# Four graph layers on one core: a projection's place in the third layer, score banks and last roots in the fourth

## The chip, the core and the metric

The kernel runs on one core of a Trainium2 chip. The metric is the device time of one execution in microseconds (us); lower is better. A core has five engines that run side by side and wait for one another by semaphores: TensorE (PE, matrix products into PSUM), VectorE (DVE), ScalarE (ACT), GpSimd (POOL) and SyncE (SP, which here only issues transfers). Each works its own list of instructions in the order in which it was given.

## The reference

Four attention layers over the same graph of 4096 nodes with 256 features, each with a residual and a layer norm. Cut to what matters for this change:

```python
# layer 1 (L0): additive attention, 4 heads, leaky slope 0.2, elu
# layer 2 (L1): 4-head dot-product attention, mask added before the softmax
# layer 3 (L2): additive attention, one head
h = x @ W
e = leaky(h @ a[:D] + (h @ a[D:]).T, 0.01)
attention = softmax(where(adj > 0, e, MASK_VAL), axis=1)
x = layernorm(x + elu(attention @ h))
# layer 4 (L3): cosine attention, values are the features themselves
Qn, Kn = cos_normalize(x @ Wq.T), cos_normalize(x @ Wk.T)
att = softmax(where(adj > 0, Kn @ Qn.T, NEG), axis=1)
x = layernorm(x + 0.5 * (att @ x) + 0.5 * x)
```

## The kernel before

The 4096 nodes are cut into 32 tiles of 128 rows. Four tiles of result rows make a block (512 columns of the transposed score matrix), so each layer runs over eight blocks, 0 to 7; within a block it runs over the 32 tiles of source nodes, in the third and fourth layer two at a time: sixteen pairs, numbered g = 0 to 15.

**Third layer** (`additive_one`). `weights(b, g)` makes the unnormalised weights of a pair: ScalarE computes a rectified row (L566) into one of two PSUM banks of the pool `pr`, VectorE turns it with the mask into `prob` (L567). From block 1 on the product with the features is done with seven half-size products instead of eight; for it VectorE (L436) and GpSimd (L437, L438) form the differences `mix`. `sums` issues the products (L446) into the four banks of `pa`, three pairs behind the weights (`LAG = 3`). After a block's last product, ScalarE and VectorE read the four banks out as `quarters` (L451 to L460), VectorE's first reading at L452; the next block's first products wait for that.

The block before is finished meanwhile: `finish(b - 1, g)` is called once in each pair. It has four row tiles k to take care of. `project` multiplies the quarters with the layer's weights (L596, four matmuls) into a bank of the pool `ps`, which has two. `take` reads that bank: a reciprocal on VectorE (L602), then an exponential and a rectification on ScalarE (L604, L605). `add` completes elu, residual and the row's statistics on VectorE (L613, L614, L156, L157). Roots and scaling follow at g = 10, 11, 14 and 15. The list of pairs in which each is called stands in `finish` by hand, since in this layer the order on TensorE, VectorE and ScalarE is the order of the program (`manual_schedule`).

Two blocks behind, the fourth layer's rows are prepared with `follow.prepare`, a generator of which one step is run in most pairs. Its matmuls L1063, at g = 8, take both banks of `ps`. Its later steps read them by ScalarE (L1070), make roots (L1073, `first_root` on ScalarE, `end_root` on GpSimd at L1076) and scale the rows (L1079).

During block 0 of the third layer, the last block of the second layer is completed by the generator `tail` (called `before` there), nineteen steps: two additions of denominators (L867), row sums on TensorE (L880) with their copies (L883), a transposition (L888), reciprocals (L903), two halves (L895, L909, L912), four row statistics, roots (on GpSimd at the end), four scalings, factors. Three steps run in each pair from g = 4.

**Fourth layer** (`cosine_attention`). `scores` multiplies a tile pair (L1118) into a bank: of `pz` (two banks), or, after block 0, of `ps` for odd tiles; ScalarE takes the exponential (L1122), VectorE the mask (L1130). The products are L446 again, four tiles behind. `pa` holds the four accumulators; the pools are opened in the order pa, pz, ps and lie in PSUM in this order, where the third layer had pr, pa, ps. Each block's `y` starts as 1.5 times the features (L1272), of which two buffers exist; `outputs_far` completes a block during the next (L1165 to L1176 and the store L1182). The third layer's last block is completed by its own tail at the start of this layer. Here a planner orders the instructions by its own estimates, apart from the end, `ending(7)`, which is in program order on TensorE, VectorE and ScalarE: for rows k = 0 to 3 it adds the last four tiles directly (`direct`, L1202) and the quarters (`others`, L1208), sums a row on ScalarE (`twice_sum`, L1213), scales and takes statistics on VectorE (`row`, L1216, L1176 to L1179), makes the roots two rows at a time (`begin_root`, `end_root`: L182, L161, L162, L168 to L171), scales by ScalarE (L1222) or VectorE (L186) and stores.

Of the kernel before, what the change touches and what calls it, by code (L numbers as in the profile page):

```python
# [9 lines left out]
FP = mybir.dt.float32  # L10
# [4 lines left out]
OP = mybir.AluOpType  # L15
# [13 lines left out]
def kernel(  # L29
# [32 lines left out]
    def pool(stack, name, bufs, **kw):  # L62
        return stack.enter_context(tc.tile_pool(name=name, bufs=bufs, reuse_waits="tile", **kw))
# [463 lines left out]
    def additive_one(w_sb, ga, tail, op, follow):  # L527

        with ExitStack() as lay:
# [87 lines left out]
            def finish(b, g):  # L617


                if g in (1, 2, 4, 6):  # L620
                    project(bank, b, g // 2)
                if g in (2, 3, 5, 7):
                    take(sb, b, g // 2 if g > 2 else 0)
                if g in (3, 4, 6, 8):
                    add(b, g // 2 - 1)
                elif g == 10:
                    roots[b] = begin_root(mvs[b])
                elif g == 11:
                    v, r, n = roots[b]
                    end_root(v, r, n, nc.gpsimd)  # L630
                    nc.gpsimd.tensor_tensor(v, mvs[b][:, :, 0], r, OP.mult)
                    nc.gpsimd.tensor_scalar(v, v, -1.0, 1.0, OP.mult, OP.add)
                elif g in (14, 15):
                    v, r, _ = roots[b]
                    for k in (2 * g - 28, 2 * g - 27):
                        y = ys[b][:, k, :]
                        nc.scalar.activation(y, y, AF.Identity, bias=v[:, k:k + 1], scale=r[:, k:k + 1])
                if g == 15:
                    if b < NB - 2:
                        far_y[b] = saved.tile([P, QB, D], FP, name=f"far_y{b}")  # L640
                        nc.scalar.dma_start(far_y[b], ys[b])
                    else:
                        nc.scalar.dma_start(X[:, b * QB:(b + 1) * QB, :D], ys[b])
# [5 lines left out]
            with tc.manual_schedule(engines=fixed):  # L649
                for i in range(len(units) + LAG):  # L650
                    b, g = units[i - LAG] if i >= LAG else (-1, 0)
                    if g == NP - 1:
                        sums(b, g)
                    if i < len(units):
                        weights(*units[i])
                    if b >= 0:
                        if g < NP - 1:
                            sums(b, g)
                        if b:
                            finish(b - 1, g)  # L660
                        else:
                            for _ in range(3 if g > 3 else 0):
                                next(before, None)
                            if g == 11:
                                follow.start()
                            elif g == 14:
                                follow.centre(bank())
                            if g % 2:
                                t = mixed[g // 2] = keep.tile([P, 2, 4, P], FP, name=f"mixed{g // 2}")
                                mix_features(t, g // 2)  # L670
                        if b > 2 and g == 0:
                            follow.prepare(bank, b - 3, 1)
                        if b > 1 and g in (2, 4, 6, 8, 9, 10, 11, 12, 13, 14, 15):
                            follow.prepare(bank, b - 2, 1, ys[b - 2])
                        if b == NB - 1 and g > 3 and g % 2 == 0:
                            q = g // 2 - 2
                            nc.scalar.dma_start(X[:, q * QB:(q + 1) * QB, :D], far_y[q])
                        if b == NB - 1 and g in (3, 5, 7):
                            follow.load_mask(0, (g - 3) // 2, prob[b, g][:, 0, :1])
# [336 lines left out]
    class Cosine:  # L1016
# [35 lines left out]
        def preparing(self, bank, b, rows):  # L1052

            in_, w_sb = self.pool, self.w_sb
            turned, squares, far = self.turning
            xT = yield from block_turning(turned, squares or self.once, far, rows, nc.sync)
            yield
            norm = in_.tile([P, QB, 2], FP, name="norm")
            rows = self.once.tile([P, QB, 2, P], FP, name="rows")
            prs = [bank().rearrange("p (t n f) -> p t n f", t=2, f=P) for _ in range(2)]  # L1060
            for k in range(QB):
                for c in range(KC):
                    nc.tensor.matmul(prs[k // 2][:, k % 2, :, :], xT[:, c, k], w_sb[:, c, :],  # L1063
                                     start=(c == 0), stop=(c == KC - 1))
            for k in range(QB):
                if k % 2 == 0:
                    yield
                for n in range(2):
                    sq = in_.tile([P, P], FP, name="sq")
                    nc.scalar.activation(sq, prs[k // 2][:, k % 2, n, :], AF.Square, accum_out=norm[:, k, n:n + 1])  # L1070
            yield
            v = in_.tile([P, QB * 2], FP, name="v")
            nc.vector.tensor_scalar_max(v, norm.rearrange("p k n -> p (k n)"), 1e-8)  # L1073
            r = first_root(v, QB * 2)
            yield
            end_root(v, r, QB * 2, nc.gpsimd)  # L1076
            for n in range(2):
                for k in range(QB):
                    nc.scalar.mul(rows[:, k, n, :], prs[k // 2][:, k % 2, n, :], r[:, 2 * k + n:2 * k + n + 1])  # L1079
                if n == 0:  # L1080
                    yield
            yield from turning_apart(self.once, self.far, lambda n: rows[:, :, n, :], lambda: self.T[b],
                                     nc.gpsimd if b < NB - 2 else nc.sync, True)
            yield
# [7 lines left out]
    def cosine_attention(co, tail):  # L1092
# [4 lines left out]
        with ExitStack() as lay:  # L1097
# [4 lines left out]
            far = pool(lay, "co_turn_far", 2, space=bass.MemoryType.DRAM)  # L1102
            co.turning = pool(lay, "co_turn", 1), None, far

            pa = pool(lay, "co_pa", 1, space=PSUM)
            pz = pool(lay, "co_pz", 2, space=PSUM)
            ps = pool(lay, "co_ps", 2, space=PSUM)
            ov = out.rearrange("(t p) d -> p t d", p=P)
            mixed, acc, prob, mix, y, back = {}, {}, {}, {}, {}, {}
# [4 lines left out]
            def scores(b, j):  # L1114
                if (b, j // MJ) not in co.mask:
                    co.load_mask(b, j // MJ)
                p = bank() if b and j % 2 else pz.tile([P, QW], FP, name="p")
                nc.tensor.matmul(p.rearrange("p (k i) -> p k i", k=QB), T[j // QB][:, 0, j % QB], T[b][:, 1],  # L1118
                                 start=True, stop=True)
                if j % 2 == 0:  # L1120
                    prob[b, j // 2] = sb.tile([P, 2, QW], FP, name="prob")
                nc.scalar.activation(prob[b, j // 2][:, j % 2, :], p, AF.Exp)  # L1122

            def weights(b, g):

# [65 lines left out]
            def ending(b):  # L1191
# [24 lines left out]
                    nc.vector.reciprocal(rden[:, k:k + 1], rden[:, k:k + 1])  # L1216
                    rest(b, k, pos[k], rden[:, k:k + 1], mv[k // 2][:, k % 2, :])

                def scaled(k, r):
                    lift = fin.tile([P, 1], FP, name=f"lift{k}")  # L1220
                    nc.vector.scalar_tensor_tensor(lift, mv[k // 2][:, k % 2, 0:1], -1.0, r[:, k % 2:k % 2 + 1], OP.mult, OP.mult)
                    nc.scalar.activation(y[b][:, k, :], y[b][:, k, :], AF.Identity, bias=lift, scale=r[:, k % 2:k % 2 + 1])  # L1222

                for k in range(2):
                    direct(k)
                first_half(c, cp.tile([P, HW], FP, name="one"), acc[b])
                second_half(c, acc[b])
                for k in range(4):
                    if k > 1:
                        direct(k)  # L1230
                    others(k)
                    twice_sum(k)
                    if k == 3:
                        scaled(0, r)
                        scaled(1, r)
                        store(b, 0, 2, nc.sync)
                        break
                    row(k)
                    if k == 1:
                        v, r, n = begin_root(mv[0])  # L1240
                        end_root(v, r, n)
                row(3)
                v, r, n = begin_root(mv[1])
                end_root(v, r, n)
                scaled(2, r)
                scale_row(y[b][:, 3, :], mv[1][:, 1:, :], r[:, 1:], 0)
                store(b, 3, 1, nc.sync)
                store(b, 2, 1, nc.scalar)

            units = [(b, j) for b in range(NB) for j in range(NT)]  # L1250
            LAG = 4
# [1 line left out]
            for i in range(len(units) + LAG):  # L1253
                if i < len(units):
                    b, j = units[i]
                    scores(b, j)
                    if j % 2:
                        weights(b, j // 2)
                    if (b, j) == (0, 3):
# [6 lines left out]
                if i >= LAG:  # L1266
# [2 lines left out]
                        acc[b] = [pa.tile([P, QW], FP, name=f"acc{n}") for n in range(4)]  # L1269
                    if j == NT - 8:  # L1270
                        y[b] = yp.tile([P, QB, D], FP, name="y")
                        nc.scalar.mul(y[b], X[:, b * QB:(b + 1) * QB, :D], 1.5)  # L1272
                    if i - LAG < len(units) - 2 * LAST:
                        for n in range(7)[:4] if j % 2 == 0 else range(7)[4:]:
                            one_product(b, j // 2, n)
# [96 lines left out]
```

## Time and profile before

| | us |
|---|---|
| median of three runs | 2808.17 (2806.68 to 2808.36) |
| the profiled execution | 2806.65 |
| its span, first to last instruction | 2804.8 |
| third layer, first product to the last before the first score | 1713.6 to 2175.5 |
| fourth layer, from its first score | 2175.6 to 2804.8 |
| last product of all (L1208) ends | 2796.7 |

Rows of the views read as follows. A wait row has who waited for whom, then the total, how often, and the longest. A timeline row has start and duration in us, the engine, the line, the operation, what it writes and reads, and how many were merged; in brackets stands the idle time in front of it and what ended it. A row of a stretch has its limits and length, then each engine's busy time with the number of instructions, the granted clock of TensorE, and the share and rate of the transfers. Matmuls overlap, so a merged row of them lasts a little longer than its issue: sixteen L1063 in a row are issued in 3.45 us (1858.26 to the next L446 at 1861.71).

### The profile page before, as it was taken

To read this page: it belongs to the slowest core of one execution; us is meant where nothing else is said; L and a number is where in the kernel's file an instruction comes from. 1 tells how busy PE (TensorE), PEld (TensorE's weight loads), DVE (VectorE), ACT (ScalarE), POOL (GpSimd) and SP (SyncE) were. 2 spreads that over 40 slices of the span, in tenths; PEclk is the share of its full clock that TensorE was granted. 3 is DMA by queue.
4 is the path that set the end of the run, shared out by engine and by line. 5 is a ranking of instruction groups with operands and counts; after the bars stand their busy time and mean duration, and the time that the engine had idled before them with its cause. 6 is when DMAs were issued, how large, how long until landed. Compare 5 with 4: busy or idle time off the path is not lost. (4 is left out here: it accounts for less than half of the span.)

```text
span 2804.8 us, 50167 instructions
## 1 busy us (share of the span) xinstructions
PE 2776.6 (99%) x19445; PEld 1428.1 (51%) x19445; DVE 2287.6 (82%) x3039; ACT 1696.5 (60%) x2648; POOL 1048.8 (37%) x982
## 2 busy tenths in 40 slices
PE   9999999999999999999999999999999999999998
PEld 5333333333443333333333333788888777777776
DVE  8899999999577788887888888888887877767676
ACT  8899999999246666666666665465556422222222
POOL 0001001000039878788788783344445100000000
PEclk9999999999999999999999999999999999999999
DMA  7566676665339899898998988567777544445442
GB/s 207 109 138 136 140 147 136 132 141 106 76 102 193 185 183 189 190 188 184 193 185 188 191 183 196 151 199 201 175 204 230 120 75 79 80 68 83 74 74 41
DMA packets 275065, 411.92 MB, mean 147 GB/s; under 512 B 54809, under 2 KB 155657, under 8 KB 273930
## 3 DMA queue, kind: packets, MB, share of 16 engines
q0 software_dynamic: 104176, 182.74, 41.1%
q1 hardware_dynamic: 164136, 218.75, 26.1%
q10 hardware_dynamic: 6514, 7.23, 0.8%
q8 instruction: 152, 2.49, 0.4%
q14 instruction: 87, 0.71, 0.1%
HBM read 335.94 MB, written 39.40 MB: 134 GB/s over the span
## 5 line engine op out<-in xcount | busy, mean ns | idle before, releaser
L834 DVE TENSOR_TENSOR prob<-p,mask 128x1024 f32<-128x1024 f32 x512 | 619.8, 1222 | 167.3 <-ACT p L824 160.1
L824 ACT ACTIVATE p<-p,shift 128x1024 f32<-128x1024 f32 x512 | 555.5, 1088 | 320.1 <-PE p L822 320.1
L312 PE MATMUL acc<-prob,V 128*32 128x512 f32 x6144 | 664.0, 593 | 1.2 <-DVE prob L302 1.2
L299 ACT ACTIVATE prob<-row,dst 128x512 f32<-128x512 f32 x1020 | 635.1, 713 | 0.6
L302 DVE SCALAR_TENSOR_TENSOR prob<-prob,mask 128x2048 f32<-128x2048 f32 x256 | 580.5, 2286 | 25.8 <-ACT prob L299 25.2
L844 POOL TENSOR_TENSOR den<-den,prob 128x1024 f32<-128x1024 f32 x220 | 556.4, 2529 | 97.2 <-DVE prob L834 84.7
L822 PE MATMUL p<-qT,kT 64*64 64x512 f32 x4096 | 531.1, 590 | 2.7 <-DVE prob L834 2.7
L858 PE MATMUL acc<-prob,V 64*64 64x512 f32 x4096 | 530.1, 589 | 0.0
L312 PEld LDWEIGHTS acc<-prob,V 128*32 128x32 f32 x6144 | 197.4, 110 | 453.0 <-issue 431.2
L446 PE MATMUL acc<-mix,mixed 128*128 128x256 f32 x1428 | 388.0, 380 | 2.7 <-DVE quarters L460 1.4
L858 PEld LDWEIGHTS acc<-prob,V 64*64 64x64 f32 x4096 | 157.3, 133 | 282.3 <-issue 280.4
L822 PEld LDWEIGHTS p<-qT,kT 64*64 64x64 f32 x4096 | 154.2, 133 | 279.8 <-issue 256.6
L446 PEld LDWEIGHTS acc<-mix,mixed 128*128 128x128 f32 x1428 | 269.7, 190 | 44.8 <-PE acc L446 3.3
L90 POOL COPY tick<-prob 128x1 f32<-128x1 f32 x35 | 38.5, 1099 | 641.8 <-DVE prob L302 641.6
L1130 DVE TENSOR_TENSOR prob<-prob,mask 128x1024 f32<-128x1024 f32 x128 | 156.2, 1220 | 147.3 <-ACT prob L1122 147.3
L850 POOL DMA_DIRECT2D den<-prob x240 | 226.1, 942 | 60.4 <-DVE prob L834 24.7
L446 PE MATMUL acc<-prob,X 128*128 128x256 f32 x952 | 245.8, 380 | 2.7 <-DVE quarters L452 2.7
L1050 POOL DMA_DIRECT2D mask<-in_adjT x64 | 47.7, 745 | 517.2 <-DVE prob L1130 430.4
L567 DVE SCALAR_TENSOR_TENSOR prob<-r,own,mask 128x512 f32<-128x512 f32 x252 | 177.1, 744 | 58.3 <-POOL mix L438 24.5
L446 PEld LDWEIGHTS acc<-prob,X 128*128 128x128 f32 x952 | 180.7, 190 | 83.5 <-issue 56.9
L1122 ACT ACTIVATE prob<-p 128x512 f32<-128x512 f32 x144 | 85.8, 598 | 196.8 <-PE p L1118 195.3
L1122 ACT ACTIVATE prob<-g 128x512 f32<-128x512 f32 x112 | 66.7, 596 | 205.1 <-PE g L1118 205.1
(229 smaller groups left out, 2818.9 us busy)
## 6 DMA issues: line engine op xcount, KB each, us to landing
mask<-in_adjT SPq DMA_DIRECT2D x254, 512.0 KB
den<-prob POOLq DMA_DIRECT2D x240, 512.0 KB, 5.3
mask<-edges SPq DMA_DIRECT2D x512, 64.0 KB
mask<-in_adjT POOLq DMA_DIRECT2D x64, 512.0 KB, 5.6
edges<-in_adj POOLq DMA_DIRECT2D x32, 512.0 KB, 9.4
far<-squares SPq DMA_DIRECT2D x16, 512.0 KB
den<-prob SPq DMA_DIRECT2D x16, 512.0 KB
row<-far SPq DMA_DIRECT2D x7, 1024.0 KB
```

The costliest lines, as they stand in the source:

```text
L299: nc.scalar.activation(z[:, h, :], r, AF.Relu, bias=-1.0, scale=dst[:, j, h:h + 1])
L302: nc.vector.scalar_tensor_tensor(z, z, 1.0, mask[m][:, j % MJ, :].unsqueeze(1).to_broadcast([P, H, QW]), OP.add, OP.mult)
L312: nc.tensor.matmul(acc[b][h * G:(h + 1) * G, n, :], part, prob[b, j][:, h, :], start=(j == 0), stop=(j == NT - 1))
L446: nc.tensor.matmul(acc[at][:, half * HW:(half + 1) * HW], w, a, start=(g == 0 and half == 0), stop=(g == NP - 1), skip_group_check=True)
L567: nc.vector.scalar_tensor_tensor(z[:, n, :], r, ga.own[:, j:j + 1], mask[:, n, :], OP.add, OP.mult)
L822: nc.tensor.matmul(p[c * d:(c + 1) * d, r, :], kT[half, c, at:at + d], qT[half, c, cols], start=True, stop=True)
L824: nc.scalar.activation(p, p, AF.Exp, bias=shift)
L834: nc.vector.tensor_tensor(z, p, mask[m][:, j % MJ, :].unsqueeze(1).to_broadcast([P, KC, QW]), OP.mult)
L844: nc.gpsimd.tensor_tensor(to, to, flat, OP.add)
L850: nc.gpsimd.dma_start(to, flat, accum_op=OP.add)
L858: nc.tensor.matmul(acc[b][c][r * d:(r + 1) * d, :], V[half, j, r * d:(r + 1) * d], prob[b, j][half, r, :], start=(j == 0), stop=(j == NH - 1))
L1130: nc.vector.tensor_tensor(z, z, co.mask[b, 2 * g // MJ][:, lo:lo + 2, :], OP.mult)
```

## The change

In the third layer the fourth projection (k = 3) is called at g = 5 instead of 6 and its `take` at g = 6 instead of 7. The steps of the second layer's tail are spread otherwise: 3 at g = 4, none at 5, then 2, 3, 4, 3 and 4 at g = 6 to 10, instead of 3 in each. In the preparing for the fourth layer, `end_root` runs on VectorE for the last two blocks. In the fourth layer the pool `pz` is opened ahead of `pa`; the product that starts `y` may not go ahead of the exponential of the tile scored in the same round; and the end is written anew: roots of rows 0 and 1 together, then of row 2, then of row 3; the first two completed by GpSimd with the shift of the mean, the last in three operations by VectorE; rows 0 to 2 scaled by ScalarE and row 3 by VectorE; all stores from the sync queue.

```diff
-                if g in (1, 2, 4, 6):
-                    project(bank, b, g // 2)
-                if g in (2, 3, 5, 7):
+                if g in (1, 2, 4, 5):
+                    project(bank, b, (g + 1) // 2 if g > 1 else 0)
+                if g in (2, 3, 5, 6):
                     take(sb, b, g // 2 if g > 2 else 0)
...
-                            for _ in range(3 if g > 3 else 0):
+                            for _ in range({4: 3, 6: 2, 7: 3, 8: 4, 9: 3, 10: 4}.get(g, 0)):
                                 next(before, None)
...
-            end_root(v, r, QB * 2, nc.gpsimd)
+            end_root(v, r, QB * 2, nc.gpsimd if b < NB - 2 else nc.vector)
...
+            pz = pool(lay, "co_pz", 2, space=PSUM)
             pa = pool(lay, "co_pa", 1, space=PSUM)
-            pz = pool(lay, "co_pz", 2, space=PSUM)
...
+                def roots(h, lo, n):
+
+                    v, r, _ = begin_root(mv[h][:, lo:lo + n])
+                    return v, r, n, mv[h][:, lo:lo + n, 0]
+
+                def lifts(v, r, n, mean):
+                    end_root(v, r, n, nc.gpsimd)
+                    nc.gpsimd.tensor_tensor(v, mean, r, OP.mult)
+                    nc.gpsimd.tensor_scalar(v, v, -1.0, 0.0, OP.mult, OP.add)
+
+                def scaled(k, v, r, n):
+                    nc.scalar.activation(y[b][:, k, :], y[b][:, k, :], AF.Identity, bias=v[:, n:n + 1], scale=r[:, n:n + 1])
...
-                for k in range(4):
-                    if k > 1:
-                        direct(k)
+                for k in range(2):
                     others(k)
                     twice_sum(k)
-                    if k == 3:
-                        scaled(0, r)
-                        scaled(1, r)
-                        store(b, 0, 2, nc.sync)
-                        break
                     row(k)
-                    if k == 1:
-                        v, r, n = begin_root(mv[0])
-                        end_root(v, r, n)
+                for k in range(2, 4):
+                    direct(k)
+                    others(k)
+                twice_sum(2)
+                both = roots(0, 0, 2)
+                row(2)
+                lifts(*both)
+                twice_sum(3)
+                third = roots(1, 0, 1)
+                scaled(0, *both[:2], 0)
+                scaled(1, *both[:2], 1)
+                store(b, 0, 2, nc.sync)
+                lifts(*third)
                 row(3)
-                v, r, n = begin_root(mv[1])
-                end_root(v, r, n)
-                scaled(2, r)
-                scale_row(y[b][:, 3, :], mv[1][:, 1:, :], r[:, 1:], 0)
+                v, r, _ = begin_root(mv[1][:, 1:])
+                scaled(2, *third[:2], 0)
+                store(b, 2, 1, nc.sync)
+                s = fin.tile([P, 1], FP, name="s_end")
+                nc.vector.scalar_tensor_tensor(s, r, v, r, OP.mult, OP.mult)
+                nc.vector.tensor_scalar(s, s, -0.5, 1.5, OP.mult, OP.add)
+                nc.vector.tensor_tensor(r, r, s, OP.mult)
+                scale_row(y[b][:, 3, :], mv[1][:, 1:], r, 0)
                 store(b, 3, 1, nc.sync)
-                store(b, 2, 1, nc.scalar)
...
-                        nc.scalar.mul(y[b], X[:, b * QB:(b + 1) * QB, :D], 1.5)
+                        with tc.issue_after(getattr(seen, "ins", seen)):
+                            nc.scalar.mul(y[b], X[:, b * QB:(b + 1) * QB, :D], 1.5)
```

`seen` is the instruction of the exponential, which `scores` now returns. `issue_after` keeps what is written under it behind that instruction on its engine.

More of the change, by code (lines that the diff above doesn't have):

```diff
@@ L1121, in scores @@
                     prob[b, j // 2] = sb.tile([P, 2, QW], FP, name="prob")
-                nc.scalar.activation(prob[b, j // 2][:, j % 2, :], p, AF.Exp)
+                return nc.scalar.activation(prob[b, j // 2][:, j % 2, :], p, AF.Exp)
             def weights(b, g):
@@ L1217, in row @@
                     rest(b, k, pos[k], rden[:, k:k + 1], mv[k // 2][:, k % 2, :])
[L1219 to L1222, printed above, removed]
+                def roots(h, lo, n):
[7 more added lines that the diff above has]
+                    nc.scalar.activation(y[b][:, k, :], y[b][:, k, :], AF.Identity, bias=v[:, n:n + 1], scale=r[:, n:n + 1])
                 for k in range(2):
@@ L1255, in cosine_attention @@
                     b, j = units[i]
-                    scores(b, j)
+                    seen = scores(b, j)
                     if j % 2:
```

## The prediction

> **What bounds the kernel now.** I read the busy line of the page first, then TensorE's waits over the whole span, then the timeline at the largest of these waits, then stretches cut at L452 (the first vector read of a finished block of the third layer), last the timeline of the end.
>
> ```profile
> PE 2776.6 (99%) x19445; PEld 1428.1 (51%) x19445; DVE 2287.6 (82%) x3039; ACT 1696.5 (60%) x2648; POOL 1048.8 (37%) x982
> ...
> PE g L1063 <- ACT h L605: 5.3, 4, 1.9
> PE acc L446 <- DVE quarters L452: 2.7, 5, 0.6
> PE g L880 <- DVE den L867: 1.6, 1, 1.6
> ...
> PE acc L446 <- POOL mix L437: 0.6, 1, 0.6
> PE g L888 <- ACT kept L883: 0.5, 1, 0.5
> ```
>
> TensorE is the bound: 2776.6 of 2804.8 us, so a change that leaves its work alone can win 28.2 us at most, some 8 of them after the last product (2796.7). The waits say where (us in total, times, longest). The one of most weight, L1063 on L605, is the fourth layer's preparing of a block, which wants two banks of `ps` and finds one still being read by `take` of the fourth projection.
>
> ```profile
> 1914.91 1.89 PE L1063 MATMUL g<-w_sb,xT 128*128 128x256 f32 x8
> 1917.22 0.16 DVE L602 RECIPROCAL rden<-g 128x1 f32<-128x1 f32 x1
> 1917.42 0.47 ACT L604 ACTIVATE e<-g,rden 128x256 f32<-128x256 f32 x1 [3.99 <-DVE rden L602]
> 1917.79 0.47 ACT L605 ACTIVATE h<-g,rden 128x256 f32<-128x256 f32 x1
> 1918.31 1.99 PE L1063 MATMUL g<-w_sb,xT 128*128 128x256 f32 x8 [1.50 <-ACT h L605]
> 1919.02 1.41 DVE L567 SCALAR_TENSOR_TENSOR prob<-r,own,mask 128x512 f32<-128x512 f32 x2 [1.63 <-POOL mix L438]
> ...
> 2035.95 3.59 PE L1063 MATMUL g<-w_sb,xT 128*128 128x256 f32 x8 [1.93 <-ACT h L605]
> ```
>
> The first eight products go, the second eight stand until L605 ends. VectorE loses 1.63 us in the same place: L567 needs L566 of its pair, which stands on ScalarE behind L604 and L605, and these wait for the reciprocal L602. (The row blames L438; in order of time it is L566, 1918.14.) After the longest wait the second eight take 3.59 us instead of 1.99.
>
> ```profile
> 1826.70:1883.30 56.60, 56.18 (x259) 48.42 (x257) 47.41 (x87) 33.70 (x75) 26.19 (x43) 1.00 0.67 185
> 1883.30:1941.80 58.50, 56.24 (x257) 48.32 (x256) 49.31 (x88) 33.65 (x75) 28.34 (x48) 1.00 0.69 193
> ...
> 2000.50:2059.40 58.90, 56.13 (x250) 48.19 (x250) 49.66 (x88) 33.60 (x75) 28.82 (x48) 0.97 0.71 192
> ```
>
> From L452 to L452, blocks 2, 3 and 5 counted from 0 (length, then busy us of each engine, the granted clock in front of the last two figures): TensorE has 56.2 us of work in each, but 3 and 5 last 58.5 and 58.9. During block b, block b - 1 is finished and b - 2 prepared.
>
> ```profile
> 2796.51 0.16 DVE L171 TENSOR_TENSOR r<-r,s 128x2 f32<-128x2 f32 x1
> 2796.59 0.16 DVE L1216 RECIPROCAL rden<-rden 128x1 f32<-128x1 f32 x1
> ...
> 2801.06 0.41 DVE L186 TENSOR_SCALAR y<-y,mv_end,r 128x256 f32<-128x256 f32 x1
> 2801.18 0.60 ACT L1222 ACTIVATE y<-y,lift,r 128x256 f32<-128x256 f32 x1 [1.02 <-DVE lift L1221]
> 2801.81 0.34 ACTq L1182 DMA_DIRECT2D out<-y  x1
> ```
>
> At the end VectorE is the chain: row 2 starts (2796.59) when the first roots are done, though its data is there at 2796.3; 3.03 us after the last store's issue the span is over.
>
> [...] 128x4 operations (L168 to L171, L631, L632) take 0.20 us and follow at 0.28, 1.6 us for six.
>
> **The change part by part** (minus is gain).
>
> *Fourth projection and take a pair earlier (third layer).* Nothing is added or removed: four matmuls of L596 (0.87 us), one L602, L604, L605 move one pair up; no DMA. The projection at g = 5 needs the bank that `take` freed at g = 3 (in this block 1901.97; TensorE gets there at 1904.98), so it doesn't wait. In pair 6 the reciprocal now comes before `add` of row 2, so VectorE has 1.96 us of L613 to L157 (1913.21 to 1915.17) to do while ScalarE does L604, L605 and L566 (0.73 + 0.76 = 1.5): the idle 1.63 of pair 7 is covered, and VectorE's chain is 1.65 us shorter. `take` ends near 1914.2, before L1063 starts at all. TensorE's losses at L1063, next L446 minus first L1063 minus 3.45: 1.78 (1914.91), 1.97, 3.75 (2032.13 to 2039.33), 0.46: 8.0. But both sides move together. L452 starts at 1826.6, 1883.3, 1941.8, 2000.5, 2059.5, 2116.9, and from the fourth reciprocal to L452 it is 24.6 us in every block, whether TensorE waited or not: VectorE's chain sets it. So blocks 3 to 5 (58.5, 58.7, 58.9) give 1.65 each: 4.95, to about 57.0, which is also TensorE's 56.2 and the waits at L452 and L460 (0.65 + 0.21). [...] Block 2 (56.7) is at that floor: 0.2. Block 6 (57.4) profits now from the late TensorE of block 5; to 57.0: 0.4. Sum **-5.6**, bounds -8.3 (every wait at L1063 gone and nothing in its place) and -1.5 (chain not shortened).
>
> *Second layer's tail spread as 3, 0, 2, 3, 4, 3, 4 steps.* Same nineteen steps. Row sums move from g = 5 to 6, behind 3.45 us of products, so L880's 1.6 + 0.1 and L888's 0.5 + 0.1 go: -2.3. Against it, the late steps bunch: VectorE has reciprocals, halves, rows and scalings (2.8, 2.1, 2.4 and 3.2 us) in g = 7 to 10 beside L567 (1.4 a pair) and the mixing (1.4 every second). I get it 1.35 us later at L590, so TensorE's first product into acc1 waits about 1 us; in return the wait on L437 in block 1 (1814.2, 0.6 and a refill, 0.9) goes, as take's 1.65 is also gained there. **-2.2**, bounds -3.2 and -0.6.
>
> *Ending.* TensorE's order is the same. ScalarE's sum of row 2 no longer stands behind the roots, VectorE's four end_root steps go to GpSimd: row 2 at 2795.45 instead of 2796.59. Row 3 then waits for TensorE (L1208 until 2796.74) and its sum: 2797.33 instead of 2798.05, over at 2798.8. GpSimd's six steps (1.6 us from 2795.9) end at 2797.6; the third row's six at 2799.5. ScalarE in order: sum 3, third root (2797.8), two scalings (2798.9), last root 2799.0 to 2799.45, scaling 2 (2800.1). VectorE: three steps of 0.2, scaling 0.41: 2800.5. Last store at 2800.5 instead of 2801.81: **-1.3**. If GpSimd is 1 us slower, ScalarE's queue passes it on: -0.3; at best -1.8.
>
> *Score banks, y's product.* pz takes the banks of `pr`, so the first scores needn't wait for L460 (2175.45). But TensorE did L596 meanwhile; between 2173.6 and 2197.0 it is busy 23.11 of 23.40 us, with some 1.4 us of broken pace. y's product (L1272, 1.06 us, which stood in front of the first exponentials for 2.0 us at 2173.2, and waited 14.9 us for stores later) now sits behind a pair's exponential; no TensorE wait came of it before. **-0.5**, bounds -1.5 and +1.5.
>
> *Roots of blocks 6 and 7 on VectorE.* Four operations of 0.16 twice, for four of 0.28 on GpSimd; ScalarE waits for them (2.7 us at L1079), TensorE doesn't: **0**, +-0.3.
>
> Sum -9.6. Against the profiled execution's 2806.65 (span 2804.8 and 1.85 around it) that is 2797.05. The runs shown have their median at 2808.17, two of three 1.5 above the profiled one; I allow 0.5 for that: **2797.5**.
>
> **Rivals.**
> 1. *TensorE alone is the limit* and the vector chain has slack: all of 8.3 at L1063, 3 in the tail, 1.5 and 1.2 at the end and in the banks: -14, 2793. For it: the 5.3 us stand in TensorE's own list. Against: the constant 24.6.
> 2. *The wait moves*: ScalarE's `take` in pair 6 only delays L566 of pair 7, the chain stays, and TensorE waits at L437 or L452 for what it no longer waits for at L1063: -1.5, -1.0, -1.0, 0: -3.5, 2803.5. For it: block 1 is at zero slack (1814.2). Against: `add` of row 2 covers it.
> 3. *Slower*: the fourth layer's order on VectorE isn't fixed by hand, and a planner that sees other banks may set the reduction L1165 earlier against its transfer. Once (2517.55) it now stands 4.61 us on `kept<-away`, and L446 behind it lost 0.54. Were it 2 us earlier in each of seven blocks, TensorE would lose 7 x 2.7 = 19: +9, 2816.5. It decides from 1.4 us a block. For it: 5 of 14 already wait. Against: nothing in these transfers is touched.
>
> **Chances.** Likeliest 0.67 (alone 2794 to 2801), rival 1 0.15, rival 2 0.12, rival 3 0.06. Range 2792 to 2803.5: from 1 us beyond rival 1 to rival 2, which leaves out rival 3 and the outer ends. 0.2% (5.6 us) is what a measurement here tells from no change: faster 0.80, within 0.14, slower 0.06.
>
> **What would show it.** No L1063 wait on L605 and no product of 0.43 there; blocks 3 to 5 near 57.0 from L452 to L452, with L452 still in TensorE's list; no L880 or L888 wait, perhaps a new one behind L591; the last store 1.3 us sooner after the last L446. Wrong if blocks stay at 58.5, or if waits on L437, L438 or L1165 grow.

## The result, and the profile after

| | before | after |
|---|---|---|
| median, us | 2808.14 (2806.51 to 2808.78, 7 runs) | 2797.55 (2795.60 to 2802.51, 7 runs) |
| ratio to before | | 0.997 (95%: 0.996 to 0.9979) |
| the profiled execution | 2806.65 | 2795.60 |
| its span | 2804.8 | 2793.8 |

The kernel is 10.6 us faster by the medians and 11.05 by the two profiled executions; the interval of the ratio stands for 5.9 to 11.2 us. From mark to mark in the two traces (us):

| stretch | before | after | difference | foretold |
|---|---|---|---|---|
| third layer's first product to its first L446 | 60.27 | 58.23 | -2.04 | -2.2 with the next row |
| to the first L452, the end of block 1 | 52.79 | 52.71 | -0.08 | |
| to the last L452 of the third layer, blocks 2 to 7 | 345.56 | 338.95 | -6.61 | -5.6 |
| to the first L452 of the fourth layer | 90.18 | 89.20 | -0.98 | -0.5 with the next row |
| to the last L446 | 525.11 | 524.94 | -0.17 | |
| to the end of the span | 17.37 | 15.97 | -1.40 | -1.3 |

The rows add up to -11.28. The third layer starts 0.25 us later in the changed kernel's trace (1713.81 us into the span, before 1713.56), which leaves the 11.05 but for rounding. TensorE's busy line on the page after:

```profile
PE 2774.1 (99%) x19445; PEld 1427.4 (51%) x19445; DVE 2289.0 (82%) x3040; ACT 1700.7 (61%) x2650; POOL 1052.5 (38%) x986
```

TensorE's waits over the whole span after (who waited for whom, total us, times, longest):

```profile
PE acc L446 <- DVE quarters L452: 3.3, 4, 1.0
...
PE acc L446 <- DVE quarters L591: 1.1, 1, 1.1
```

The list no longer has L1063, L880 or L888. The wait behind L591, VectorE's last copy of block 0's result, is new, and L452 remains: TensorE still arrives at a block's end sooner than VectorE lets it go on. Block 3 shows why the wait at L1063 went. VectorE's timeline after:

```profile
1907.04 0.16 DVE L602 RECIPROCAL rden<-g 128x1 f32<-128x1 f32 x1
1908.84 1.41 DVE L567 SCALAR_TENSOR_TENSOR prob<-r,own,mask 128x512 f32<-128x512 f32 x2 [1.64 <-POOL mix L438]
...
1910.89 0.16 DVE L602 RECIPROCAL rden<-g 128x1 f32<-128x1 f32 x1
1910.97 0.41 DVE L613 SCALAR_TENSOR_TENSOR e<-e,h 128x256 f32<-128x256 f32 x1
...
1912.92 1.41 DVE L567 SCALAR_TENSOR_TENSOR prob<-r,own,mask 128x512 f32<-128x512 f32 x2
```

and TensorE's (the next L446 starts at 1916.03):

```profile
1912.58 3.62 PE L1063 MATMUL g<-w_sb,xT 128*128 128x256 f32 x16
```

The fourth reciprocal (1910.89) is followed by the addition of row 2 (from 1910.97), and the next L567 starts without idle time at 1912.92: ScalarE did L604, L605 and L566 beside the addition. All sixteen L1063 go in one piece. The third reciprocal (1907.04) has no such cover: in front of the L567 at 1908.84 the same idle time of 1.64 us is still there. The stretches from L452 to L452, blocks 3 to 6 (length, then busy time of each engine, clock, transfers):

```profile
1881.00:1938.00 57.00, 56.48 (x259) 48.53 (x257) 49.42 (x89) 33.79 (x75) 28.48 (x48) 1.00 0.74 199
1938.00:1995.00 57.00, 55.90 (x256) 48.33 (x256) 49.42 (x88) 33.76 (x75) 28.40 (x48) 1.00 0.76 199
1995.00:2051.60 56.60, 55.67 (x256) 48.39 (x256) 49.01 (x88) 33.79 (x75) 29.10 (x48) 1.00 0.74 200
2051.60:2108.90 57.30, 56.37 (x258) 48.31 (x256) 49.72 (x88) 33.80 (x75) 29.01 (x48) 1.00 0.72 197
```

Blocks 3 to 5 lost 1.5 to 2.3 us against 58.5 to 58.9, block 6 only 0.1 (57.4 to 57.3). The end after, in order of time:

```profile
2785.68 0.15 DVE L1216 RECIPROCAL rden<-rden 128x1 f32<-128x1 f32 x1
...
2787.63 0.16 DVE L1216 RECIPROCAL rden<-rden 128x1 f32<-128x1 f32 x1 [0.34 <-ACT one L1213]
...
2787.72 0.19 POOL L1227 TENSOR_SCALAR v<-v 128x2 f32<-128x2 f32 x1
...
2789.76 0.22 DVE L1258 SCALAR_TENSOR_TENSOR s_end<-r,v 128x1 f32<-128x1 f32 x1 [0.51 <-ACT r L162]
...
2790.39 0.41 DVE L186 TENSOR_SCALAR y<-y,mv_end,r 128x256 f32<-128x256 f32 x1
```

Counted from the last L446 (2787.47 before, 2777.83 after), row 2 starts at 7.85 us (foretold 7.98), row 3 at 9.80 (9.86), GpSimd's first six steps end at 10.08 (10.13), and the last scaling ends at 12.97 (13.03).

### The profile page after: what moved, and what is told of

It reads as the page before. It is cut to its first block, busy times and chain, and to the rows that moved or that the text cites. A ratio compares the mean times of both kernels' runs of the same rounds, so it can differ in the third digit from the quotient of the medians.

```text
span 2793.8 us, 50176 instructions
## 1 busy us (share of the span) xinstructions
PE 2774.1 (99%) x19445; PEld 1427.4 (51%) x19445; DVE 2289.0 (82%) x3040; ACT 1700.7 (61%) x2650; POOL 1052.5 (38%) x986
## 5 line engine op out<-in xcount | busy, mean ns | idle before, releaser
L446 PE MATMUL acc<-mix,mixed 128*128 128x256 f32 x1428 | 388.0, 380 | 2.7 <-DVE quarters L460 1.2
L446 PEld LDWEIGHTS acc<-mix,mixed 128*128 128x128 f32 x1428 | 269.5, 190 | 45.0 <-PE acc L446 3.5
L850 POOL DMA_DIRECT2D den<-prob x240 | 232.0, 967 | 61.0 <-DVE prob L834 22.3
L446 PE MATMUL acc<-prob,X 128*128 128x256 f32 x952 | 245.7, 380 | 3.4 <-DVE quarters L452 3.3
L446 PEld LDWEIGHTS acc<-prob,X 128*128 128x128 f32 x952 | 180.1, 190 | 84.1 <-issue 56.7
L567 DVE SCALAR_TENSOR_TENSOR prob<-r,own,mask 128x512 f32<-128x512 f32 x252 | 177.1, 744 | 51.3 <-POOL s L169 13.7
```

Source lines behind the costliest of these rows:

```text
L446: nc.tensor.matmul(acc[at][:, half * HW:(half + 1) * HW], w, a, start=(g == 0 and half == 0), stop=(g == NP - 1), skip_group_check=True)
L567: nc.vector.scalar_tensor_tensor(z[:, n, :], r, ga.own[:, j:j + 1], mask[:, n, :], OP.add, OP.mult)
L850: nc.gpsimd.dma_start(to, flat, accum_op=OP.add)
```

## The experiments

Each kernel ran beside the kernel before on the same chip. The ratio is to that, with its 95% interval; "blocks 2 to 7" is the sum from L452 to L452 of the third layer in the run's trace.

**The take a pair earlier, alone.** The kernel before with the two lists of `finish` changed:

```diff
-                if g in (1, 2, 4, 6):
-                    project(bank, b, g // 2)
-                if g in (2, 3, 5, 7):
+                if g in (1, 2, 4, 5):
+                    project(bank, b, (g + 1) // 2 if g > 1 else 0)
+                if g in (2, 3, 5, 6):
```

> The kernel before with the third layer's two lists alone (fourth projection at g = 5, its take at g = 6). Theory (the vector chain sets the length of blocks 3 to 5 and is 1.65 us shorter): 5.5 to 6.6 us faster than before; from L452 to L452 57.0 us in blocks 3 to 5 instead of 58.5 to 58.9; no wait of L1063 on L605; the wait of L446 on L437 in block 1 gone; L452 waits stay or grow to about 1 us. Rival 1 (TensorE's own waits are the limit): 8 us and more, blocks at 56.5. Rival 2 (the wait moves): 2 us or less.

Measured: 2801.05 us, ratio 0.9979 (0.9971 to 0.9987): 5.9 us, as expected. Blocks 2 to 7 take 338.61, as in the changed kernel (338.95): the whole gain of the third layer's blocks comes from these lists. No wait of TensorE at L1063 is left, and L452 has 3.6 us. The wait on L437 in block 1, which was to go, is 0.33 us instead of 0.62.

**The tail's spread, alone.**

```diff
-                            for _ in range(3 if g > 3 else 0):
+                            for _ in range({4: 3, 6: 2, 7: 3, 8: 4, 9: 3, 10: 4}.get(g, 0)):
```

> The kernel before with the second layer's tail spread as 3, 0, 2, 3, 4, 3, 4 steps alone. Theory: the waits at L880 and L888 (2.1 us and refills) go, a new wait of about 1.3 us on L591 comes, and the wait on L437 in block 1 changes by less than 1: in all 1 to 2 us faster. Rival (all steps hidden, nothing in return): 2.3 us or more and no wait on L591.

Measured: 2805.61 us, ratio 0.9998 (0.999 to 1.0007). The median is 1.3 us lower, but by the interval that is not told from none. The waits at L880 and L888 are gone, as foretold, and L446 starts 58.32 us after the layer's first product (58.23 in the changed kernel). But the first block with L446 then lost 2.5 us. TensorE's timeline of this run:

```profile
1774.19 0.83 PE L446 MATMUL acc<-mix,mixed 128*128 128x256 f32 x2 [2.16 <-DVE quarters L591]
1774.81 1.06 PE L446 MATMUL acc<-mix,X 128*128 128x256 f32 x2
1775.67 1.06 PE L446 MATMUL acc<-mix,mixed 128*128 128x256 f32 x2
```

TensorE waits 2.16 us for VectorE's copy L591, and the pairs of products after it take 0.86 us from start to start instead of 0.43. The fourteen products from 1774.81 on take 4.60 us, where the same ones take 3.02 in the changed kernel (1775.06 to 1778.08): 1.58 us more. Counted from the layer's first product (1712.26 here, 1713.81 in the changed kernel), TensorE comes to this place at 59.8 us here and 59.7 there, but is let go at 61.9 here and at 60.7 there: VectorE is later, and its timeline in this run shows where that begins:

```profile
1750.51 1.41 DVE L567 SCALAR_TENSOR_TENSOR prob<-r,own,mask 128x512 f32<-128x512 f32 x2 [1.14 <-DMA mask<-in_adjT]
```

The mask's transfer came late for one L567; in the changed kernel the same L567 (1750.84) has no wait in front of it, and up to L591 the list of VectorE is the same in both. All seven other traces with this spread have 0.9 to 1.1 us at L591. So the 2.2 us and the slower products behind them belong to this one execution, not to the tail alone. The gain at L880 is real, and how much of it is kept depends on where VectorE stands at the next meeting of the two engines.

**TensorE's wait taken away, the take left where it was.** L1063 goes one pair later, to g = 9, so that it finds its banks free; the two steps behind it, in which ScalarE squares and sums what L1063 wrote (L1070), then run together at g = 10:

```diff
-                        if b > 1 and g in (2, 4, 6, 8, 9, 10, 11, 12, 13, 14, 15):
-                            follow.prepare(bank, b - 2, 1, ys[b - 2])
+                        if b > 1 and g in (2, 4, 6, 9, 10, 11, 12, 13, 14, 15):
+                            follow.prepare(bank, b - 2, 2 if g == 10 else 1, ys[b - 2])
```

> The kernel before, with the fourth projection and take left where they were, and L1063 one pair later instead (g = 9, the squares of all four rows then together at g = 10). TensorE then finds both banks free, and VectorE's chain through take isn't shortened. Theory (the chain sets the pace): the L1063 wait goes from TensorE's list, but blocks 3 to 5 stay within 0.7 us of 58.5 and the wait comes up at L452 or L437: 0 to 2.5 us faster[...]. Rival 1 (TensorE's waits are the limit): about 7 to 8 us faster.

Measured: 2812.22 us, ratio 1.002 (1.0012 to 1.0029), slower. TensorE's waits of this run:

```profile
PE acc L446 <- ACT one L451: 6.2, 5, 1.9
PE acc L446 <- DVE quarters L452: 5.1, 6, 1.0
```

The wait at L1063 is gone, and as much and more stands at the end of the blocks, which take 59.2 us where the kernel before has 58.5 to 58.9. The vector and scalar chain became longer by some 0.4 us a block, and VectorE's timeline in block 4 shows the place:

```profile
1992.26 1.41 DVE L567 SCALAR_TENSOR_TENSOR prob<-r,own,mask 128x512 f32<-128x512 f32 x2 [3.30 <-POOL v L632]
```

In the kernel before this wait is 2.27 us. (The row blames L632; in order of time it is L566, which starts on ScalarE at 1991.34, behind eight L1070 instead of four.) So the experiment freed TensorE and also put 1.03 us into VectorE's chain. Had that chain had slack, as rival 1 says, the blocks would have shortened all the same; they became longer. Rival 1 falls.

**The fourth layer's part, alone.** The changed kernel with the lists and the tail's spread as before (one of the two edits is the reverse of the first diff, the other of the second).

> The kernel after without both edits of the third layer (lists and tail as before): all of the fourth layer's edits alone. Theory: 1.4 us from the new end and about 1.0 from the start of the layer: 2 to 3 us faster, in the last L446 to the end of the span 16.0 instead of 17.4 us. With the two runs above the sum should be that of the whole change, about 10 to 11. Rival (the parts need each other): the sum is short by 2 us or more.

Measured: 2805.98 us, ratio 0.9998 (0.999 to 1.0006), not told from none, where 2 to 3 us were expected. The end takes 15.97 us instead of 17.37, and so the 1.40 is there; but TensorE lost 2.4 us once in the middle of the fourth layer, of which more below. With the old lists, block 6 of this run:

```profile
2058.70:2117.70 59.00, 56.20 (x257) 48.31 (x256) 49.82 (x89) 33.71 (x75) 28.91 (x48) 1.00 0.73 192
```

Block 6 has 59.0, as block 5 has (58.9). In the profiled execution of the kernel before it had 57.4. VectorE's timeline there, in block 5 and at the same place of block 6:

```profile
2010.97 1.73 DVE L504 CUSTOM_DVE_ANT_0 h<-X,a_row 128x256 f32<-128x256 f32 x1
...
2069.70 0.41 DVE L504 CUSTOM_DVE_ANT_0 h<-X,a_row 128x256 f32<-128x256 f32 x1
```

L504 is a row of dot products for the next block. Beside the first, GpSimd's L438 and L437 run for 1.69 us of its time, beside the second for 0.19. In the kernel before, the L504 of blocks 2 to 6 take 0.39 us with no such work beside them, 0.41 to 0.42 with 0.19 to 0.20 us of it, 0.75 to 0.77 with 0.47 to 0.49, 0.94 to 1.19 with 0.66 to 1.08, and 1.72 to 1.73 with 1.68 to 1.69. This makes 1.3 of the 1.5 us; the same term is in block 5's 56.6 in the changed kernel (1.04 us in place of 1.73). That GpSimd's work is the cause was not tested by a run.

**The next idle time of the same kind.** The changed kernel, the addition of row 1 in the pair of the third reciprocal:

```diff
-                if g in (3, 4, 6, 8):
-                    add(b, g // 2 - 1)
+                if g in (3, 5, 6, 8):
+                    add(b, (g - 2) // 2)
```

> The changed kernel with the addition of row 1 alone in pair 5 instead of pair 4. Theory (vector chain): q1 to q7 loses 2 to 3 us, the waits of L446 on L452 (3.3 us in all) fall below 1.5; the L591 wait of 1.1 stays; 2795. Rival (the chain isn't what is left): q1 to q7 stays within 0.5 of 338.95, 2797.5.

Measured: 2792.07 us, ratio 0.9949 (0.9937 to 0.9962): 14.2 us below the kernel before on this chip, where the changed kernel was 10.6 below it on its own; the intervals of the two ratios just touch. Blocks 2 to 7 take 334.50, 4.45 less. VectorE's timeline of this run in block 3:

```profile
1907.44 0.16 DVE L602 RECIPROCAL rden<-g 128x1 f32<-128x1 f32 x1
1907.52 0.40 DVE L613 SCALAR_TENSOR_TENSOR e<-e,h 128x256 f32<-128x256 f32 x1
...
1909.47 1.41 DVE L567 SCALAR_TENSOR_TENSOR prob<-r,own,mask 128x512 f32<-128x512 f32 x2
```

and two of its stretches, blocks 4 and 6:

```profile
1934.50:1990.60 56.10, 56.10 (x261) 49.12 (x260) 49.97 (x88) 33.71 (x75) 28.53 (x48) 1.00 0.80 202
...
2046.90:2102.80 55.90, 55.52 (x256) 48.07 (x255) 49.97 (x89) 33.74 (x75) 29.09 (x48) 1.00 0.76 202
```

The 1.64 us are covered, each of blocks 3 to 6 loses another 0.3 to 1.6, and TensorE, busy for 56.10 of 56.10 us and 55.52 of 55.90, is the limit at last. The vector chain was what set these blocks, before the change and after it. The 2 to 3 us expected in blocks 2 to 7 were too few: the floor was put at 56.2 to 56.3 us a block, and blocks 3 to 6 take 55.9 in the mean.

**That, and two steps of the tail drawn forward.** The diff above and

```diff
-                            for _ in range({4: 3, 6: 2, 7: 3, 8: 4, 9: 3, 10: 4}.get(g, 0)):
+                            for _ in range({4: 3, 6: 2, 7: 3, 8: 6, 9: 1, 10: 4}.get(g, 0)):
```

> The changed kernel with two more edits that follow from the theory that VectorE's chain sets a block of the third layer: the third addition (row 1) goes from pair 4 to pair 5, and in the second layer's tail a step of pair 9 and one more are drawn forward into pair 8 (6 and 1 instead of 4 and 3). Theory (the vector chain sets L452, TensorE's own 56.2 us are the floor just below): blocks 3 to 5 from 56.6 to 57.0 go to 56.3, the whole q1 to q7 of 338.95 loses 2 to 3 us, the 1.1 us wait of L446 on L591 goes or shrinks below 0.3: 3 to 4 us faster than the changed kernel, near 2794, ratio to before 0.995. Rival (TensorE's broken pace and waits on L452 that come from ScalarE's quarters, not the vector chain, are what is left): blocks stay at 56.6 to 57.0, 0 to 1 us faster, 2797.

Measured: 2788.69 us (2787.27 to 2792.94), ratio 0.994 (0.9928 to 0.9953), whose interval lies below that of the changed kernel: the best here, 17.6 us below the kernel before on this chip, where about 14 were expected. The kernel with the pools in the old order, below, ran on the same chip and has 2797.51. Blocks 2 to 7 take 333.45, and the wait behind L591 fell from 1.1 us to 0.2. The runs of this kernel and of the one above overlap, so what the two steps of the tail add is not shown by the medians.

**The start of the fourth layer, four kernels.** The pools in the old order:

```diff
-            pz = pool(lay, "co_pz", 2, space=PSUM)
             pa = pool(lay, "co_pa", 1, space=PSUM)
+            pz = pool(lay, "co_pz", 2, space=PSUM)
```

> The changed kernel with the fourth layer's pools in the old order (the four accumulators before pz). Theory (the banks are what starts the first scores earlier, but TensorE has other work anyway): from the last L452 of the third layer to the first of the fourth 89.2 becomes 89.5 to 90.2, 0.3 to 1.0 us slower, 2798. Rival (the 1.0 us there comes from y's product being held back): 89.2 stays, 2797.5.

y's product free to go ahead:

```diff
-                        with tc.issue_after(getattr(seen, "ins", seen)):
+                        if True:
```

> The changed kernel without the rule that the product which starts y (L1272 before) may not go ahead of the exponential of its round. Theory (the banks made the 1.0 us): 89.2 stays from the last L452 of the third layer to the first of the fourth, the rest within 0.5: 2797.5. Rival (y's product in front of the first exponentials is what cost): 90.0 or more, 2798.5. Should the product stand in front of an exponential later in the layer and TensorE wait for it, fourth L452 to last L446 grows over 525.5.

Both of these together:

> The changed kernel with both the old order of the pools and without the rule on y's product. Theory (each of the two alone takes away most of the broken pace at the fourth layer's start, since the other stands in for it): from the last L452 of the third layer to the first of the fourth 90.0 to 90.3 as before the change. Rival (most of the 1.0 us comes from the roots of the last two blocks on VectorE): 89.5 to 89.7, as with the pools alone. The whole: 2798, 0.3 to 1 us over the changed kernel, below what a look can tell.

The roots of the last two prepared blocks on GpSimd:

```diff
-            end_root(v, r, QB * 2, nc.gpsimd if b < NB - 2 else nc.vector)
+            end_root(v, r, QB * 2, nc.gpsimd)
```

> The changed kernel with the roots of the last two prepared blocks on GpSimd again. Theory (ScalarE waits for them, TensorE doesn't): 89.2 from the last L452 of the third layer to the first of the fourth, 54.8 from the sixth to the seventh L452 of the third layer, all as in the changed kernel, 2797.5. Rival (they are the 1.0 us): 89.9 to 90.2.

Measured, with the time from the last L452 of the third layer to the first of the fourth (89.20 in the changed kernel):

| | us | ratio | L452 to L452 |
|---|---|---|---|
| pools in the old order | 2797.51 | 0.9969 (0.9958 to 0.9979) | 89.54 |
| y's product free | 2795.61 | 0.9964 (0.9952 to 0.9977) | 88.98 |
| both | 2799.18 | 0.997 (0.996 to 0.9979) | 89.34 |
| roots on GpSimd | 2797.19 | 0.9969 (0.9953 to 0.9985) | 89.29 |

None brings the 90.18 of the profiled execution before back, so every theory of the 1.0 us named here falls; the pools alone stand at the lower edge of what was expected of them (89.5 to 90.2). The first three kernels above settle it: they have the whole old fourth layer and each shows 89.28. The 0.9 us belong to that one execution, not to the change; these edits are worth some 0.1 us there (the pools alone 0.3), no more than such traces differ by.

**The wait that varies.** The run with both undone lost 5 us in the fourth layer's middle. SyncE's issues, VectorE's and TensorE's timeline of it there:

```profile
2504.36 0.55 SPq L1158 DMA_DIRECT2D kept<-away  x1
```

```profile
2503.99 0.69 DVE L436 TENSOR_TENSOR mix<-prob 128x512 f32<-128x512 f32 x1
2512.79 0.69 DVE L1165 TENSOR_REDUCE rden<-kept 128x2 f32<-128x512 f32 x1 [8.11 <-DMA kept<-away]
2513.39 0.41 DVE L437 TENSOR_TENSOR mix<-prob,mix 128x256 f32<-128x256 f32 x1
```

```profile
2513.86 1.30 PE L446 MATMUL acc<-mix,mixed 128*128 128x256 f32 x4 [4.05 <-DVE mix L437]
2514.96 1.92 PE L1118 MATMUL g<-T,T 128*128 128x512 f32 x2
```

The reduction L1165 stands between L436 and L437 of a pair, and its transfer came 8.4 us after its issue; in the changed kernel's trace it came 5.4 us after. VectorE then stood 4.43 us and TensorE 0.4, here 8.11 and 4.05, with slower products after it (two L1118 in 1.70 us from start to start instead of 0.86). This is the place of rival 3, but not its mechanism: the reduction isn't set much earlier against its transfer (VectorE comes to it 0.3 us after the issue here, 1.0 in the changed kernel, 1.1 in the kernel before), the transfer took longer. TensorE's wait is in the kernel before too (0.54 us). In the four traces with the old fourth layer it is 0.3 to 0.9; in the eight with edits of that layer and the reduction not held it is 0 to 4.1, in four of them above 1. Whether the change makes the long waits more frequent, so few traces can't tell. Held behind a later pair's L438, in the changed kernel (the call of `outputs_far` at tile 14 instead of 10, and):

```diff
-        eng.tensor_tensor(s[:, 3, :], z[:, 1, :HW], s[:, 2, :], OP.subtract)
+        return eng.tensor_tensor(s[:, 3, :], z[:, 1, :HW], s[:, 2, :], OP.subtract)
...
-                    nc.vector.tensor_reduce(rden[:, 2 * h:2 * h + 2], back[b, h], AX.X, OP.add)
+                    with tc.issue_after(mixed_last[0]) if h else nullcontext():
+                        nc.vector.tensor_reduce(rden[:, 2 * h:2 * h + 2], back[b, h], AX.X, OP.add)
```

> The changed kernel with the second reduction of the statistics in the fourth layer (L1165) held behind the mixing of a pair some three pairs later, so that VectorE doesn't stand in front of its transfer. Theory (the runs' spread of 7 us and the missing 2 us of the sum of parts are this wait: 4.4 to 8.1 us of VectorE in block 3, of which TensorE loses 0.4 to 4.1): no wait of TensorE on L437 near 2510, fourth L452 to last L446 at 524.2 to 524.6 in the profile, all runs within 4 us, median 1 to 2 us under the changed kernel, 2795.5 to 2796.5. Rival [...]: spread stays near 7 us, median 2797.5. Third: ten operations in a bunch behind the reduction delay the mask by 3 us once a block and TensorE waits for it: 1 to 5 us slower.

Measured: 2796.18 us (2793.34 to 2796.95), ratio 0.9958 (0.9945 to 0.997). TensorE's wait on L437 there is gone, and from the fourth layer's first L452 to the last L446 it is 524.00 us; the bunch behind the reduction costs TensorE nothing. The runs spread over 3.6 us instead of 6.9. With all three of these edits:

> The kernel with the later addition and the drawn-forward tail, which had 2788.7, with the reduction held as well. Theory: 1 to 2 us less, 2787, runs within 4 us. Rival: 2788.7 with the same spread as before (5.7 us).

Measured: 2789.82 us (2789.32 to 2792.22), ratio 0.9941 (0.9927 to 0.9954). The spread is 2.9 us instead of 5.7, but the median isn't lower: its profiled execution has 524.01 in the fourth layer, and 1.6 us of TensorE at L895 <- L903 in block 0, a wait that the run with two edits doesn't have; ahead of it an L567 stood 2.62 us for its mask's transfer. Against the kernel before on their own chips, holding the reduction gives 11.2 us instead of 10.6 on the changed kernel and 17.6 instead of 17.6 on the other: a gain in the median is not shown. That the wait goes is, and the smaller spread rests on five runs each.

## Why the prediction was right, and where its sizes were off

*Fourth projection and take: the mechanism right, the size too small.* Foretold -5.6, in the two traces -6.61. The step was that VectorE's chain sets L452, so that 1.65 us a block come and not what TensorE stands. It is shown from three sides: the lists alone give it, freeing TensorE at the price of 1.03 us in the chain makes the blocks longer, and shortening the chain once more gives 4.45 more. VectorE's idle time in each of blocks 3 to 6 tells the same: 9.2 us before, 10.2 with the preparing later, 7.6 in the changed kernel, 5.9 to 6.3 with the addition later. Before, none of its waits of over 0.25 us in these blocks ends with a product of TensorE. Off was the term for block 6, "to 57.0: 0.4": the sum was made on an execution in which that block had 57.4, and put it down to the late TensorE of block 5; in VectorE's list it is the short L504. In the two other traces with the old lists that weren't otherwise altered in these blocks (the tail alone, the fourth layer alone) it has 58.9 to 59.0, and blocks 2 to 7 take 346.75 and 347.10. Against these the lists bring 7.8 to 8.2 us, close to the bound of -8.3 given; by the medians the lists alone give 5.9 (3.6 to 8.1 by the interval).

*The floor.* "To about 57.0, which is also TensorE's 56.2 and the waits at L452 and L460" counted those waits as a fixed part. They weren't: they belonged to the same chain, and with another idle time covered the blocks went to 55.5 to 56.3.

*Tail's spread: -2.2 foretold, -2.12 in the pair of traces.* The new wait behind L591 was foretold at about 1 us and has 1.1. For the tail alone no gain is shown: its interval holds none. The 2.2 us at L591 come from a late mask in that trace (1.14 us of VectorE), and 1.58 us more were lost in the products behind them.

*Ending: -1.3 foretold, -1.40 measured,* with each of its steps within 0.15 us. GpSimd's first six operations took 1.58 us, where 1.6 were foretold.

*Score banks and y's product: -0.5 foretold, some -0.1 shown.* The term took the 1.4 us of broken pace at that place for a property of the kernel. Other traces of the same fourth layer don't have 0.9 of it. *Roots on VectorE: 0 foretold,* 0.1 at most seen.

*The whole.* That the median of 2797.55 us lies so near the 2797.5 foretold is luck. The parts were summed to -9.6 from one execution, and 0.5 was added to the time for the later median. The pair of traces has -11.05: the take brought 1.0 more, and the fourth layer's start 0.5 more, which is the slow start of that one execution before. The parts run alone add up to -5.9 - 1.3 - 1.0 = -8.2 by the medians, where about 10 to 11 were expected and a sum short by 2 us or more was to speak for parts that need each other. The 2.4 missing can't be told from none, since each part's interval is over 2 us wide on either side; what the traces of the parts alone lost in slower products (1.2 to 1.6 us) and at L1165 (2.4 us) is of that size, but single traces can't apportion medians.

*The rivals.* Rival 1 fell with the preparing put later. Rival 2, the wait that moves, is what that experiment did, not the change. Rival 3's place was right, its mechanism and its price were not: not 2.7 us in each of seven blocks, but 0 to 4.1 in one block, by a transfer that took 5.4 to 8.4 us from its issue, and with the pools in the old order as well as in the new.

## What to carry to other kernels

A wait of the busiest engine may be only where two chains meet: before taking it away, compare the period of the loop in iterations with the wait and without, and look for the idle time in the chain that sets the period. Here VectorE's idle time between a reciprocal and the instruction that waits for ScalarE behind it was 1.64 us; an addition beside it gave 1.5 to 2.3 us in each of blocks 3 to 5 the first time, and 0.3 to 1.6 in each of blocks 3 to 6 the second. And a difference of under 1 us in one stretch of one trace is to be seen in a second trace of the same code before it gets a term in a sum.

## What the runs showed of the hardware

After some of its waits TensorE's products took up to twice their usual time for a while. In the kernel before, eight L1063 behind a wait of 1.93 us took 3.59 us instead of 1.99. Four L581 took 3.39 us instead of 1.88 behind 1.76 us at L880 (the take alone), and five took 3.54 behind 1.66 us there (the fourth layer alone), where six take 2.74 in the kernel before; pairs of L446 took 0.86 us instead of 0.43 behind 2.16 us at L591 (the tail alone), and two L1118 took 1.70 us instead of 0.86 soon after 4.05 us at L437 (the pools in the old order and y's product free). But in the kernel before three L581 behind 1.61 us at L880 took 1.45 us and eight L1063 behind 1.69 us took the usual 1.99, and in the run of the fourth layer alone two L1118 soon after 2.43 us at L437 took the usual 0.86 from start to start. No length of a wait divides the two cases in these traces. The loss was 1.2 to 1.7 us each time, nearly as much again as the shorter of these waits. The runs don't show what decides, nor that the wait is the cause.

VectorE's L504 is four times as long beside GpSimd's L437 and L438 (1.73 us) as without (0.39), and this one instruction made 1.3 us of a block's length. That the overlap is the cause is read from the traces and was not tested.
